# A recurrence woven into a layer stack: its input loads issued 16 steps earlier than before, the scaling of the inputs kept where it was

## The chip, the cores and the metric

The kernel runs on one core of a Trainium2 chip. A core has five engines that run at the same time, each taking its own instructions in order: TensorE (PE, with its weight loads shown as PEld), VectorE (DVE), ScalarE (ACT), GpSimd (POOL) and SyncE (SP). SP computes nothing here; it issues transfers between the chip's memory and the core's on-chip memory. An instruction that waits for another engine or for a transfer waits on a semaphore, and holds everything behind it on its own engine.

The metric is the device time in microseconds of one execution. Beside it there is one execution that was profiled, with its own time and the span from its first to its last instruction.

## The reference, cut to what matters

The model has two layers of the form "token mixer, then feed-forward part". What the change touches is the feed-forward part of layer 0, a recurrence over 4096 tokens for 4 batch entries and 128 channels:

```python
B, T, H = (x.shape[0], x.shape[1], W.shape[0])      # 4, 4096, 128
Wx = jnp.einsum('bti,hi->bth', x, W)
flat = Wx.reshape(B * T, H)
mean = jnp.mean(flat, axis=0)
var = jnp.var(flat, axis=0)
Wx = ((flat - mean) * jax.lax.rsqrt(var + BN_EPS) * gamma + beta).reshape(B, T, H)
def step(yt, wx_t):
    yt = jax.nn.sigmoid(wx_t + yt @ Vt)
    return (yt, yt)
_, ys = jax.lax.scan(step, y0, jnp.swapaxes(Wx, 0, 1))
```

Its result is added to the layer's input. The mixer of layer 1 takes the sum: eight layers of a selective state-space model (Mamba) over the same tokens, each with its own projections, a short convolution, a scan over the tokens for 256 channels and 16 states, and a gate:

```python
for l in range(DEPTH):                               # 8
    seq = _mamba_layer(seq, W_in[l], conv_w[l], ...)
    seq = _rmsnorm(seq, rms_w[l])
```

Before this stand the mixer of layer 0 (an attention over windows with sampled positions), and behind it the feed-forward part of layer 1 (a routed set of experts). Neither is touched.

## The kernel before, in words

The kernel keeps channels on the 128 partitions and tokens along the free dimension. Its order of work is written out by hand: each engine's instructions stand in the order in which the Python code issues them, and a framework adds the semaphore waits that the data need. Four parts follow each other: the attention mixer (`conv_layer`), the set-up and first steps of the recurrence, the eight Mamba layers with the rest of the recurrence woven in (`mamba`), and the experts.

**The recurrence** (class `Recurrence`, from L605). A group is 64 steps (`RT`). `load(n)` allocates two tiles of 128 x 4 x 64 numbers in fp32 from a pool of two buffers each, and issues two transfers on SP: `wx`, the projected inputs (L664), and `x1`, the layer's input that is added at the end (L666). Each reads 128 KB in runs of 256 bytes. At the end of `load` one ScalarE instruction (L667) scales and shifts `wx` by the batch statistics, in place. `step(t)` is a product of the state with the matrix V on TensorE (L683), into a PSUM tile that at the first step of a group was filled with the scaled inputs (L678). `tanh(t)` is a ScalarE instruction (L691) on 128 x 4 numbers that gives the next state. At the last step of a group POOL turns the states into outputs, writing them into the `wx` tile (L697), adds `x1` (L698), and SP stores the sum (L700).

**Where the loads stood.** `tanh(t)` called `load(n + 1)` at step 32 of group n, just after that step's tanh. So the two transfers and the scaling were issued together, and stood on SP and ScalarE at the place of step 32.

**The first 576 steps** (nine groups) run alone, each step waiting for the one before it. Small dummy products fill TensorE between them (L655).

**The eight layers.** The tokens are cut into eight chunks of 512. A *body* is one chunk, one layer and one batch entry: 8 x 8 x 4 = 256 bodies, batch entry innermost, so that body number modulo 4 is the batch entry b. A body has 16 slots, each with two scans on DVE (L1075) for one pair of states and one half of the channels. For these, ScalarE makes the decay factors `dA` (L1020), three slots ahead, and TensorE the inputs `dBx` (L1042), one slot ahead. POOL multiplies four states at a time by the C coefficients (L1100), and TensorE adds up the products (L1104). A table (`PLAN`) places the other pieces of the next body and the previous one: projections, convolution taps (L895, L898, L904), gates, norms (L838 to L841 for a chunk's first layer), stores and fetches.

Another table, `STEPS`, places 16 recurrence steps in each body, at most two in a slot. After the first 576 steps, 3520 remain, which takes 220 bodies. A group of 64 steps therefore spans exactly four bodies: step 0 falls on the first slot of a body with b=0, step 16 on that of b=1, step 32 on that of b=2.

**SP's queue in a body.** SP issues in this order: copies of the C coefficients, spread over all partitions, 1 MB each (`Cb`, L957, four for each body, of which the first two go out in the last slots of the body before it); the weights of the next layer at the start of bodies with b=1 (`given`, L828, 640 KB); and later in the body the small transfers that hold coefficients for the next body (L942, L1009), B (L950) and the spread diagonal (`diag`, L1014, 1.8 MB). In the last layer of a chunk there are also stores of the result (L1167), loads of the value it is added to (L1159), and the next chunk's inputs (L834).

Of the kernel before, what the change touches and what calls it, by code (L numbers as in the profile page):

```python
# [10 lines left out]
AF = mybir.ActivationFunctionType  # L11
# [12 lines left out]
L = H * W  # L24
# [30 lines left out]
RT = 64  # L55
# [6 lines left out]
class Ops:  # L62


    def __init__(self, nc, const):
        self.nc = nc
        self.ident = const.tile([P, P], F32, name="ident")
        make_identity(nc, self.ident)
        self.avg = const.tile([P, P], F32, name="avg")
        nc.vector.memset(self.avg, 1.0 / P)  # L70
        self.one = const.tile([P, 1], F32, name="one")
        nc.vector.memset(self.one, 1.0)
        self.eps5 = const.tile([P, 1], F32, name="eps5")
        nc.vector.memset(self.eps5, 1e-5)
        self.eps6 = const.tile([P, 1], F32, name="eps6")
        nc.vector.memset(self.eps6, 1e-6)
# [533 lines left out]
class Recurrence:  # L610
# [5 lines left out]
    def __init__(self, ctx, tc, ops, I, stats, wx_d, x1_d, x2_d):  # L616
        nc = self.nc = tc.nc
        self.ops, self.wx_d, self.x1_d, self.x2_d = ops, wx_d, x1_d, x2_d
        c = ctx.enter_context(tc.tile_pool(name="rc", bufs=1))
        self.w = ctx.enter_context(tc.tile_pool(name="rw", bufs=2))  # L620
        self.ps = ctx.enter_context(tc.tile_pool(name="rps", bufs=1, space=PSUM))
        vt = self.vt = c.tile([P, P], F32, name="vt")
        nc.sync.dma_start(out=vt, in_=I["V"])
        vec = c.tile([P, V_N], F32, name="vec")
        nc.sync.dma_start(out=vec, in_=I["vec"])
        nc.vector.tensor_scalar(vt, vt, 0.5, None, ALU.mult)
        mv = c.tile([P, 2], F32, name="mv")
        nc.vector.bn_aggr(mv, stats.rearrange("p n s -> p (n s)"))
        sc = self.sc = c.tile([P, 1], F32, name="sc")
        ops.rstd(sc, mv[:, 1:2], ops.eps5)  # L630
        nc.scalar.preload_act_table_set(EXP_TANH)
        nc.vector.tensor_tensor(sc, sc, vec[:, V_GAMMA : V_GAMMA + 1], ALU.mult)
        sh = self.sh = c.tile([P, 1], F32, name="sh")
        nc.vector.tensor_tensor(sh, mv[:, 0:1], sc, ALU.mult)
        nc.vector.tensor_tensor(sh, vec[:, V_BETA : V_BETA + 1], sh, ALU.subtract)
        self.still = c.tile([P, P], BF16, name="still")
        nc.gpsimd.memset(self.still, 0.0)
        idle = self.ps.tile([P, TL], F32, tag="p", name="idle")
        for _ in range(32):
            self.busy(idle, TL // P)  # L640
        half = self.ps.tile([P, RT, B], F32, tag="p", name="half")
        nc.tensor.matmul(half[:, 0, 0:1], vt, ops.one, start=True, stop=True)
        idle = self.ps.tile([P, TL], F32, tag="p", name="idle")
        for _ in range(6):
            self.busy(idle, TL // P)
        nc.vector.tensor_tensor(sh, sh, half[:, 0, 0:1], ALU.add)
        z0 = c.tile([P, B], F32, name="z0")
        nc.vector.memset(z0, -1.0)
        self.before = z0
        self.got = {}  # L650
        self.load(0)

    def busy(self, out, n):

        self.nc.tensor.matmul(  # L655
            out[:, : n * P].rearrange("p (n t) -> p n t", n=n), self.still,
            self.still.unsqueeze(1).to_broadcast([P, n, P]), start=True, stop=True,
        )

    def load(self, n):  # L660
        nc = self.nc
        here = (slice(None), slice(None), slice(n * RT, (n + 1) * RT))
        wx = self.w.tile([P, B, RT], F32, tag="wx", name="wx")
        nc.sync.dma_start(out=wx, in_=self.wx_d[here])  # L664
        x1 = self.w.tile([P, B, RT], F32, tag="x1", name="x1")
        nc.sync.dma_start(out=x1, in_=self.x1_d[here])  # L666
        nc.scalar.activation(wx, wx, AF.Identity, scale=self.sc, bias=self.sh)  # L667
        self.got[n] = wx, x1

    def step(self, t):  # L670

        nc = self.nc
        n, k = divmod(t, RT)
        if k == 0:

            self.wx, self.x1 = self.got.pop(n)
            self.p = self.ps.tile([P, RT, B], F32, tag="p", name="p")
            nc.tensor.matmul(  # L678
                self.p, self.ops.ident, self.wx.rearrange("p b t -> p t b"), start=True, stop=False,
                skip_group_check=True,  # L680
            )
            self.z = self.w.tile([P, RT, B], F32, tag="z", name="z")
        nc.tensor.matmul(  # L683
            self.p[:, k, :], self.vt, self.before, start=False, stop=True, skip_group_check=True
        )

    def tanh(self, t):

        nc = self.nc
        n, k = divmod(t, RT)  # L690
        nc.scalar.activation(self.z[:, k, :], self.p[:, k, :], AF.Tanh, scale=0.5)  # L691
        self.before = self.z[:, k, :]
        if k == RT // 2 and n + 1 < L // RT:
            self.load(n + 1)
        if k == RT - 1:
            y = self.wx
            nc.gpsimd.tensor_scalar(y, self.z.rearrange("p t b -> p b t"), 0.5, 0.5, ALU.mult, ALU.add)  # L697
            nc.gpsimd.tensor_tensor(self.x1, self.x1, y, ALU.add)  # L698
            here = (slice(None), slice(None), slice(n * RT, (n + 1) * RT))
            nc.sync.dma_start(out=self.x2_d[here], in_=self.x1)  # L700
# [46 lines left out]
def mamba(tc, ops, I, rec, x2_d, x3_d):  # L747
# [16 lines left out]
    with ExitStack() as ctx:  # L764
# [438 lines left out]
        def side(who, j, part):  # L1203

            for k, what in plan[j][part] if part < len(plan[j]) else ():
                if who.get(k):
                    pieces[what](who[k])

        load(0)
        idle = psf.tile([P, TL], F32, tag="f0", name="idle")  # L1210
        for t in range(PRE):
# [10 lines left out]
        for i in range(-2, len(bodies) + 1):  # L1222
# [7 lines left out]
            if o and o.b == 1 and i + 3 < len(bodies):  # L1230
                load(bodies[i + 3].l)
# [466 lines left out]
```

## Time and profile before

| What | Value |
|---|---|
| Time, median of 3 runs | 14895.22 us (14884.57 to 14900.8) |
| Profiled execution, its time | 14892.08 us |
| Profiled execution, span | 14890.3 us |
| Busy share of PE, DVE, ACT, POOL | 95%, 87%, 74%, 85% |
| Mean granted TensorE clock | 0.984 |
| First scan of the first body to last scan of the last | 1946 to 14607 us |
| L667, scaling | 64 executions, 0.60 us each |
| L664, load of wx: issue to landing, whole program | 2.5 / 7.4 / 13.5 us (min, median, max) |
| L666, load of x1: issue to landing, whole program | 2.4 / 7.2 / 12.7 us (min, median, max) |

The page gives busy time per engine, the span in 40 slices, the transfers, and the costliest groups of instructions. Views of the trace behind it give who waited for whom, the instructions in order of time, and busy times in chosen stretches. A busy share is an average over the stages. Idle time of an engine matters only where another engine, or the end, waits for it.

### The profile page before, as it was taken

Reading aid. Unit: us, or ns where it says so; the run is one execution under the profiler, and the core shown is the slowest. Engines: PE = TensorE matmul, PEld = TensorE weight load, DVE = VectorE, ACT = ScalarE, POOL = GpSimd, SP = SyncE. Lnnn points to the kernel's source line nnn. Section 1 sums busy time; section 2 is a strip of 40 time slices with the busy share of each in tenths; the row PEclk is TensorE's granted clock in tenths of the full one; section 3 lists DMA queues with packets and bytes.
Section 4 is the critical chain, followed back from the end, with each engine's and each line's share of the span. In section 5 each row is a group of like instructions: output and inputs, shape, how many; then the busy total and the mean of one; then the engine's idle time right before and its main releaser. Section 6 shows DMA issues by size and latency. Waiting matters only on the chain. (4 is left out here: it accounts for less than half of the span.)

```text
span 14890.3 us, 307789 instructions
## 1 busy us (share of the span) xinstructions
PE 14160.7 (95%) x124378; PEld 10821.2 (73%) x124378; DVE 12974.0 (87%) x16043; ACT 10980.2 (74%) x21400; POOL 12589.8 (85%) x5760
## 2 busy tenths in 40 slices
PE   7999989999999999999999999999999999999996
PEld 3444467777777777777777777777777777777775
DVE  8997079998999899999998999989999999989994
ACT  6887267777777777777777777777777777777773
POOL 5564079999999999999999999999999999999993
PEclk8999999999999999999999999999999999999998
DMA  0000034434443434343444344344434343434344
GB/s 23 26 26 23 29 122 144 144 136 148 142 147 135 152 137 150 132 151 138 149 142 144 137 149 142 138 145 145 146 136 151 138 149 133 154 131 145 133 146 184
DMA packets 600044, 1914.56 MB, mean 129 GB/s; under 512 B 347488, under 2 KB 347872, under 8 KB 434272
## 3 DMA queue, kind: packets, MB, share of 16 engines
q1 hardware_dynamic: 598480, 1894.60, 36.1%
q8 instruction: 984, 16.12, 0.4%
q14 instruction: 436, 3.57, 0.1%
q10 hardware_dynamic: 144, 0.26, 0.0%
HBM read 1823.10 MB, written 71.57 MB: 127 GB/s over the span
## 5 line engine op out<-in xcount | busy, mean ns | idle before, releaser
L1100 POOL TENSOR_TENSOR hs<-hs,Cb 128x2048 f32<-128x2048 f32 x2048 | 9300.9, 4543 | 749.0 <-DVE state L1092 562.3
L1075 DVE TENSOR_TENSOR_SCAN hs<-dA,state,dBx 128x512 f32<-128x512 f32 x7168 | 8808.2, 1267 | 700.2 <-PE dBx L1042 561.3
L1020 ACT ACTIVATE dA<-dt,A 128x512 f32<-128x512 f32 x7168 | 4730.4, 716 | 11.6 <-DVE hs L1075 5.5
L1104 PE MATMUL yT<-ident,hs 128*128 128x128 f32 x32768 | 4376.9, 277 | 30.4 <-POOL hs L1100 30.2
L1042 PE MATMUL dBx<-diag,dtxT 64*128 64x128 f32 x57344 | 4195.3, 283 | 27.1 <-DVE hs L1075 20.1
L1104 PEld LDWEIGHTS yT<-ident,hs 128*128 128x128 f32 x32768 | 3785.4, 147 | 433.6 <-issue 349.2
L1042 PEld LDWEIGHTS dBx<-diag,dtxT 64*128 64x128 f32 x57344 | 3509.4, 187 | 800.7 <-issue 741.3
L683 PEld LDWEIGHTS p<-z,vt 128*128 128x128 f32 x8192 | 1283.9, 189 | 881.8 <-ACT z L691 401.8
L691 ACT ACTIVATE z<-p 128x4 f32<-128x4 f32 x4096 | 702.3, 171 | 1396.6 <-PE p L683 1368.8
L683 PE MATMUL p<-z,vt 128*128 128x4 f32 x8192 | 1453.7, 248 | 107.1 <-ACT z L691 98.4
L1075 DVE TENSOR_TENSOR_SCAN hs<-dAp,state,hs 128x512 f32<-128x512 f32 x1024 | 1273.3, 1273 | 296.7 <-POOL hs L1063 296.7
L1063 POOL TENSOR_TENSOR hs<-Bb,dtx 128x512 f32<-128x512 f32 x1024 | 1284.9, 1280 | 0.0
L904 DVE SCALAR_TENSOR_TENSOR xc<-f,taps,xc 128x511 f32<-128x511 f32 (+2 forms) x1536 | 1115.8, 726 | 53.4 <-ACT z L691 49.3
L1020 ACT ACTIVATE dAp<-dt,A 128x512 f32<-128x512 f32 x1024 | 708.8, 692 | 491.6 <-DVE hs L1075 470.1
L279 DVE SCALAR_TENSOR_TENSOR acc<-qp,dww,acc 128x512 f32<-128x512 f32 x1184 | 892.4, 754 | 25.6
L979 POOL TENSOR_TENSOR dtx<-dt,xc 128x512 f32<-128x512 f32 x512 | 651.6, 1273 | 217.5 <-ACT dt L973 217.5
L293 POOL TENSOR_TENSOR off<-off,to 128x512 f32<-128x512 f32 x288 | 366.4, 1272 | 412.7 <-ACT to L291 400.0
L1020 ACT ACT_TABLE_LOAD x511 | 655.6, 1283 | 9.0
L898 ACT ACTIVATE xc<-f,taps 128x512 f32<-128x512 f32 x512 | 350.7, 685 | 414.7 <-PE f L895 281.1
L919 PE MATMUL f<-u,given 128*128 128x512 f32 x1024 | 600.6, 670 | 3.8 <-DVE xc L904 3.8
L847 PEld LDWEIGHTS f<-avg,sq 128*128 128x128 f32 x2048 | 257.0, 197 | 466.0 <-ACT sq L1148 466.0
L895 PE MATMUL f<-u,given 128*128 128x512 f32 x1024 | 567.0, 636 | 0.8 <-DVE u L868 0.8
(235 smaller groups left out, 15160.8 us busy)
## 6 DMA issues: line engine op xcount, KB each, us to landing
Cb<-c_d SPq DMA_DIRECT2D x1024, 1024.0 KB, 7.2
diag<-spare SPq DMA_DIRECT2D x256, 1792.0 KB, 8.8
Bb<-c_d SPq DMA_DIRECT2D x256, 512.0 KB, 4.8
given<-in_m_given_dram SPq DMA_DIRECT2D x64, 640.0 KB, 8.6
slab<-in_w_dram SPq DMA_DIRECT2D x60, 512.0 KB, 9.9
x<-x_d SPq DMA_DIRECT2D x96, 256.0 KB, 3.0
c_d<-dbl SPq DMA_DIRECT2D x512, 32.0 KB, 1.6
x_d<-x SPq DMA_DIRECT2D x63, 256.0 KB, 3.2
```

What stands on the lines that cost most here:

```text
L279: nc.vector.scalar_tensor_tensor(rows(to), x, dww[:, t : t + 1], rows(o.acc), ALU.mult, ALU.add)
L683: nc.tensor.matmul(self.p[:, k, :], self.vt, self.before, start=False, stop=True, skip_group_check=True)
L691: nc.scalar.activation(self.z[:, k, :], self.p[:, k, :], AF.Tanh, scale=0.5)
L904: nc.vector.scalar_tensor_tensor(x, o.v[h][:, : TL - k], taps[:, o.l, h, DC - 1 - k : DC - k], x, ALU.mult, ALU.add)
L919: nc.tensor.matmul(o.pz[h], o.given[:, at : at + P], o.u, start=True, stop=True)
L979: nc.gpsimd.tensor_tensor(to, blocks(o.dt[h]), blocks(o.xc[:, h, :]), ALU.mult)
L1020: nc.scalar.activation(o.dA[j][:, k, :], o.dt[h], AF.Exp, scale=A[:, o.l, h, n : n + 1])
L1042: nc.tensor.matmul(o.dBx[j][:, at : at + 64, :], o.dtxT[h][row, n, :], o.diag[row, n, :, 2 * sp : 2 * sp + 2], start=True, stop=True,)
L1063: nc.gpsimd.tensor_tensor(hs[:, k, :].rearrange("p (q n t) -> p q n t", n=NB, q=2), o.Bb[:, k, :].rearrange("p (q n t) -> p q n t", n=NB, ...
L1075: nc.vector.tensor_tensor_scan(hs[:, k, :], o.dA[j][:, k, :], hs[:, k, :] if sp == SP_B else o.dBx[j][:, :, k], state[:, o.l, o.b, h, s : ...
L1100: nc.gpsimd.tensor_tensor(hs, hs, o.Cb[f], ALU.mult)
L1104: nc.tensor.matmul(o.yT[:, n, :], x[:, n * P : (n + 1) * P], ops.ident, start=start and n == 0, stop=True, is_transpose=True, skip_group_c ...
```

## The change

`load` no longer ends with the scaling. The scaling is a function of its own, `scale(n)`. The constructor calls both, one after the other, for group 0. In the steps, `load(n + 1)` is called at step 16 of a group and `scale(n + 1)` at step 32.

```diff
         self.load(0)
+        self.scale(0)
...
         x1 = self.w.tile([P, B, RT], F32, tag="x1", name="x1")
         nc.sync.dma_start(out=x1, in_=self.x1_d[here])
-        nc.scalar.activation(wx, wx, AF.Identity, scale=self.sc, bias=self.sh)
         self.got[n] = wx, x1
+
+    def scale(self, n):
+        wx = self.got[n][0]
+        self.nc.scalar.activation(wx, wx, AF.Identity, scale=self.sc, bias=self.sh)
...
         self.before = self.z[:, k, :]
-        if k == RT // 2 and n + 1 < L // RT:
-            self.load(n + 1)
+        if n + 1 < L // RT:
+            if k == RT // 4:
+                self.load(n + 1)
+            if k == RT // 2:
+                self.scale(n + 1)
```

## The prediction

> **What bounds the kernel now.** I read the page first: its rows of engines and slices show a kernel that is nearly full from 1946 us on, so only time that stops several engines at once can be won. Then I read the waits of ScalarE (ACT), because the change touches what ACT waits for. Columns: engine and tile, "<-" what it waited for, total us, times, longest us. Over the eight-layer stage (window 1900 to 12900 us, the whole part in which recurrence steps are woven into the layers):
>
> ```profile
> ACT z L691 <- PE p L683: 1090.6, 1532, 6.6
> ACT dAp L1020 <- DVE hs L1075: 304.3, 405, 3.2
> ...
> ACT wx L667 <- DMA wx<-wx_d: 88.3, 45, 7.5
> ```
>
> The third line is the scaling at step 32: 45 of its 54 executions here wait for the load issued just ahead of them, 88.3 us in all. Over the window before (1490 to 1900 us, the steps alone) the only wait of L667 is the set-up's:
>
> ```profile
> ACT wx L667 <- DVE z L648: 2.3, 1, 2.3
> ```
>
> There SP has nothing else to do and has issued each load as soon as its buffer was free, long before ACT comes to it. So those nine loads can give nothing.
>
> An ACT wait is not yet lost time. I therefore cut the stage into bodies, from one body's first scan (L1075) to the next one's. A body holds 16 steps, so the load at step 32 always falls on the third body of a layer (b=2), and step 16 on the second (b=1). Lengths from the trace: b=1 and b=3 take 48.57 us in layers 0 to 6 and 50.70 us in layer 7 (which also prepares the next chunk), nearly without exception. Bodies b=2 do not. Five stretches (length, busy time per engine with counts, granted clock of PE, DMA share, GB/s):
>
> ```profile
> 3418.18:3477.28 59.10, 52.50 (x460) 42.58 (x459) 46.57 (x55) 38.67 (x75) 47.30 (x21) 0.94 0.39 136
> 3477.28:3527.98 50.70, 49.71 (x460) 40.04 (x459) 46.55 (x55) 38.29 (x74) 47.25 (x21) 1.00 0.43 150
> 5553.03:5601.63 48.60, 47.58 (x446) 38.35 (x445) 45.14 (x52) 37.78 (x73) 45.15 (x19) 1.00 0.42 156
> 5601.63:5650.20 48.57, 47.55 (x446) 38.34 (x445) 45.12 (x52) 38.26 (x74) 45.11 (x19) 1.00 0.41 140
> 2631.68:2682.93 51.25, 49.19 (x446) 39.20 (x445) 45.33 (x52) 38.06 (x74) 45.09 (x19) 0.97 0.38 134
> ```
>
> Rows 1 and 2 are b=2 and b=3 of one layer 7: same work, 8.40 us apart. Row 4 is a b=2 whose load was in time (wait 0), as long as row 3, its neighbour without a load; the 0.60 us of the scaling itself is hidden, ACT being busy 38 of 48.6 us. Row 5 is a b=2 with a wait of 2.07 us. In the long ones PE's clock was granted at 0.94 and 0.97 in place of 1.00, so the idle stretch also slows PE afterwards. This is why a body can lose more than ACT waited.
>
> Why the load is late stands in the order of time of the b=2 of row 1 (SP's issues, then ACT's work; start, length, instruction):
>
> ```profile
> 3415.74 0.32 SPq L1159 DMA_DIRECT2D x<-x_d  x1
> 3416.11 0.43 SPq L834 DMA_DIRECT2D x<-x_d  x1
> 3416.59 0.90 SPq L957 DMA_DIRECT2D Cb<-c_d  x2
> 3417.53 0.57 SPq L664 DMA_DIRECT2D wx<-wx_d  x1
> ...
> 3428.13 0.60 ACT L667 ACTIVATE wx<-wx,sh,sc 128x256 f32<-128x256 f32 x1 [7.50 <-DMA wx<-wx_d]
> ...
> 3429.98 0.75 DVE L904 SCALAR_TENSOR_TENSOR xc<-f,taps,xc 128x511 f32<-128x511 f32 x1 [5.50 <-ACT z L691]
> ```
>
> The load goes out behind two 1 MB copies of C (L957) and lands 0.5 us after the second of them, 10.6 us after its issue. ACT stands at L667 and holds the activations behind it: L841, L898, the next tanh and the dA exponentials. DVE then idles 5.50 us for the L898 result. In layers 0 to 6 the load is issued 3.9 us before the body, its C copies in front of it, and lands at +1.5 to +4.5 us; ACT reaches L667 at +2.35.
>
> **The change, part by part.**
> *Removed: the wait of L667.* The instruction keeps its place on ACT at step 32. Its load will have gone out at about -3.5 us of b=1, and ACT reaches L667 at +2.35 of b=2: 54 us later (48.6 + 5.9). The slowest landing of L664 in this stage, 11.3 us from issue, leaves 43 us of that.
> What that is worth, body by body (length of each loaded b=2 less its floor):
> - Layers 0 to 6, 48 bodies, floor 48.57. In the 23 with a wait under 1 us the mean excess is 0.00: the queue of prepared exponentials absorbs it. In the 11 with 1 to 1.5 us it is 0.87 us, in the 14 with more, 1.35 us: 11 x 0.87 + 14 x 1.35 = 28.5.
> - Layer 7, 6 bodies, floor 50.70 (their b=1 and b=3): 59.10 + 59.72 + 57.66 + 61.22 + 60.42 + 57.52 - 6 x 50.70 = 51.4. Waits there: 5.9 to 7.5 us.
> - Together 79.9 us. That it comes near the 88.3 of the wait row is chance: short waits cost nothing, long ones more than their length.
>
> *Added: one method call; no instruction.* In program order both kernels have the same instructions at the same places on PE, ACT, DVE and POOL; on SP 54 pairs of L664 and L666 stand one body earlier, behind the weight load `given` (L828), ahead of the third C copy. The round of eight DMA semaphores shifts, so that some instructions name another predecessor; each named one was issued eight transfers earlier and has landed.
>
> *Moved: two issues on SP.* They take SP 1.2 us in b=1 as a rule (0.57 and 0.63), 2.9 at worst (1.25 and 1.64), from 3.5 us before the body. SP's next is the C copy at +0.7 us, which waits for POOL anyway, so nothing behind them is late. Neither waits at its new place: the buffers come free with POOL's L698 and the store L700, which is landed by +7.5 us of body b=0 at the latest, over 40 us ahead. No POOL queue is passed.
>
> *Moved: 256 KB of transfers.* In b=1 they stand behind `given` and ahead of C copy 3. I bound what they push back: from nothing (C copy 3 lands at +6.7 us behind them in b=2, at +7.0 without them in b=3) to 1 us (x1 lands 0.46 us behind wx, so twice that). C copy 3 in b=1 lands at +8.0 and is used by POOL at +19.9, with at least 10.3 us of room; copy 4 at least 13.7. I take nothing. In b=2 the C copies lose this traffic, which matters to nobody.
>
> **A rule against the rows.** The Trainium skill, "DMA: Bandwidth & Descriptors", section "Anatomy of one DMA — SWDGE (gpsimd) path", fits a transfer as 2.0 us plus bytes over 436 GB/s (for that path; this is SP's). For 131072 bytes I estimate 2.3 us. Issued 3.9 us before the body, wx would land at -1.6 and nobody would wait: by the rule the change is worth almost nothing outside layer 7, and there (issue at -0.65, landing at +1.7, ACT at +2.45) nothing either, so 14895. With an empty queue the trace agrees (2.5 us at best), but in this stage the row says 5.4/7.5/11.3 us (min, median, max). The same page's "Queues, rings and completion order" says why: each DMA engine takes its descriptors in ring order, and here 2 MB of C stand ahead. The row decides.
>
> **Sum.** Profiled execution: span 14890.3, time 14892.1. Less 79.9: span 14810.4, time 14812.2. The median of the runs is 3.1 above the profiled time: 14895.2 - 79.9 = 14815.3.
>
> **Rivals.**
> 1. *Part of the layer-7 gain stays away* (14840 to 14866). There the C copies 1 and 2 themselves are late in b=2, since L1159 has to wait for a store to land (issue at -2.4, landing of copy 1 up to +6.6 us). With ACT freed POOL wants copy 1 at +8.4, so the room shrinks to 1.8 us. If another wait took that place, up to 51.4 would remain lost: 14866. Against it: b=3 of layer 7 has the same late copies (up to +6.3) and takes 50.70.
> 2. *No change* (within 30 us, about 14890): the time is lost elsewhere and the wait only displays it. Against: excess is zero in every body with no wait or a short one.
> 3. *Slower, crowding in b=1.* The moved loads use 256-byte runs; the same page ("Specifications") sets 512 bytes as the least for full rate. If they held up C copy 3 by more than its 10.3 us of room, POOL would stall in each of 54 bodies. Two us past that point is 108 us, a net 28 slower (14923); the break-even is 11.8 us of delay. The 0.46 us between wx and x1 speaks against it, but the mix with `given` is untried.
> 4. *More gain* (14790 to 14805): the 36 bodies after the last step run in an irregular pattern (48.3 to 51.4 us) that a different entry could shift by some 10 to 20 us, either way.
>
> **How the numbers follow.** Likeliest case 0.79, with its own range 14805 to 14830; rival 1 0.09, rival 2 0.04, rival 3 0.04, rival 4 0.04. A change of 0.2% (30 us) is about what can be told from no change. The low end takes in part of rival 4 and the high end most of rival 1: 14800 to 14845. Faster (likeliest, rival 4, most of rival 1) 0.91; within 0.2% 0.05; slower 0.04.
>
> **What would show it.** L667's wait for the DMA gone; b=2 at 48.57 and 50.70 us with PE's clock at 1.00; b=1 unchanged; wx landing at about +6 us of b=1. The forecast is wrong if b=1 grows, if a wait on POOL's C copies appears, or if layer-7 b=2 bodies stay above 51 us.

## The result

The changed kernel takes 14814.31 us (median of 4 runs, 14813.63 to 14817.47); the kernel before takes 14893.86 us (median of 4, one run more than above). The ratio is 0.9948, with a 95% interval of 0.9932 to 0.9964: faster by 79.6 us, about half a per cent. The forecast was 14815.3.

In lines of `kernel.py` the change moves what stands behind it: the scaling L667 is now L672, the loads L664 and L666 are L665 and L667, the tanh L691 is L695, the C copies L957 are L964. (The class of the recurrence begins at L610; the description above gives L605.)

ScalarE's waits in the changed kernel over the layers (window 1900 to 12900 us; columns: what waited, for what, total us, times, longest us):

```profile
ACT z L695 <- PE p L687: 1096.3, 1563, 6.9
ACT dAp L1027 <- DVE hs L1082: 294.9, 403, 3.2
ACT dbl L946 <- PE f L940: 251.9, 224, 2.4
```

The first two stand where they stood (1090.6 and 304.3 us). The 88.3 us of the scaling are gone; it has no row any more. What stood behind it shows on DVE. In the same window, the waits of the convolution's taps for ScalarE's result, before:

```profile
DVE xc L904 <- ACT z L691: 49.3, 73, 5.5
```

and after:

```profile
DVE xc L911 <- ACT z L695: 9.5, 48, 0.5
```

Next come four bodies of the changed kernel that answer to those shown of the one before (length, busy time per engine, granted clock, DMA share, GB/s). The first two are b=2 and b=3 of the first layer 7, the last two b=1 and b=2 of a middle layer:

```profile
3415.94:3466.67 50.73, 49.74 (x460) 40.05 (x459) 46.57 (x55) 38.78 (x75) 47.29 (x21) 1.00 0.44 149
3466.67:3517.37 50.70, 49.72 (x460) 40.07 (x459) 46.55 (x56) 38.32 (x74) 47.24 (x21) 1.00 0.43 150
5531.11:5579.70 48.59, 47.57 (x446) 38.35 (x445) 45.13 (x52) 37.78 (x73) 45.14 (x19) 1.00 0.43 155
5579.70:5628.26 48.56, 47.54 (x446) 38.34 (x445) 45.10 (x52) 38.26 (x74) 45.11 (x19) 1.00 0.39 140
```

The body of 59.10 us is now one of 50.73, with PE's clock at 1.00 throughout. ScalarE's work in it is the same: 38.78 us of activity, against 38.67.

In order of time the same stretch reads as follows (SP's issues at the start of b=1 and of b=2, then ScalarE's):

```profile
3361.36 0.43 SPq L835 DMA_DIRECT2D given<-in_m_given_dram  x1
3361.84 0.56 SPq L665 DMA_DIRECT2D wx<-wx_d  x1
3362.44 0.63 SPq L667 DMA_DIRECT2D x<-x_d  x1
...
3413.66 3.29 SPq L964 DMA_DIRECT2D Cb<-c_d  x3
...
3418.23 0.17 ACT L695 ACTIVATE z<-p 128x4 f32<-128x4 f32 x1 [0.89 <-PE p L687]
3418.30 0.59 ACT L672 ACTIVATE wx<-wx,sh,sc 128x256 f32<-128x256 f32 x1
```

The loads go out right behind the weights, 56 us ahead of the scaling. The C copies of b=2 still come late, but the scaling follows its tanh without a gap.

Over all 54 loaded groups, bodies b=2 now take 48.57 us in layers 0 to 6 (48.55 to 48.59) and 50.81 in layer 7 (50.70 to 51.23). Cut the spans at the first scan and at the body after the last step: of the difference of 74.6 us between the two profiled spans (14890.3 and 14815.7), b=2 gave 79.2, the other bodies of this stretch took back 2.5, the part ahead of the first body took 2.9 more, and the remaining 36 bodies and the experts gave 0.8. So the bodies b=2 account for the whole gain.

### The profile page after: what moved, and what is told of

Read it like the earlier page. It is cut to its first block, busy times and chain, and to the rows that moved or that the text cites. A ratio compares the mean times of both kernels' runs of the same rounds, so it can differ in the third digit from the quotient of the medians.

```text
span 14815.7 us, 307842 instructions
## 1 busy us (share of the span) xinstructions
PE 14124.4 (95%) x124378; PEld 10790.5 (73%) x124378; DVE 12971.0 (88%) x16043; ACT 10985.9 (74%) x21400; POOL 12590.3 (85%) x5760
## 5 line engine op out<-in xcount | busy, mean ns | idle before, releaser
L695 ACT ACTIVATE z<-p 128x4 f32<-128x4 f32 x4096 | 703.1, 172 | 1403.9 <-PE p L687 1374.6
```

## The experiments

Times are medians; the kernel before took 14891 to 14899 us beside them. Where a body's excess is named, it is its length less 48.57 us, or less 50.70 us in layer 7. The diffs are against the changed kernel, except the seventh, which is against the kernel before; they show the lines that matter, with constants written as numbers.

**1. The loads stay, the scaling moves.** This parts the wait from the traffic.

```diff
-            if k == RT // 4:
+            if k == RT // 2:
                 self.load(n + 1)
-            if k == RT // 2:
+            if k == 3 * RT // 4:
                 self.scale(n + 1)
```

> Both loads stay at step 32, as in the kernel before; only the scaling moves, to step 48. Theory (time is lost where ScalarE stands at the scaling until wx has landed, and nowhere else): the wait is gone, bodies b=2 take 48.57 us in layers 0 to 6 and 50.7 in layer 7, b=3 the same; 14815 us, give or take 10. Rival A (the gain comes from moving 256 KB of transfers out of b=2): the traffic stays, so about 14890. Rival B (the C copies in layer 7 hold b=2 up by themselves): b=2 of layer 7 stays above 55 us, some 14865.

Measured: 14811.25 us (ratio 0.9944, 0.9927 to 0.9960). All b=2 bodies are at their floors (48.58 and 50.72 on average), and b=3, where the scaling now stands, too. The transfers are where they always were, so it was not their traffic (rival A) and not the late C copies of layer 7 (rival B).

**2. Only the awaited load moves.** The load of x1 is split from `load` into a function of its own, called at step 32:

```diff
             if k == RT // 2:
+                self.load_x1(n + 1)
                 self.scale(n + 1)
```

> As after the change, but x1, which nobody waits for before the end of its group, is loaded at step 32 again; wx alone at step 16. Theory: 14815 us, no wait of the scaling. Rival A (moved traffic): half of it is back in b=2, so half of the gain is lost, about 14855.

Measured (one run): 14812.82 us, b=2 at 48.61 and 50.71. That x1 moves along does nothing, for good or ill.

**3. Load and scaling both at step 16.**

```diff
-            if k == RT // 2:
+            if k == RT // 4:
                 self.scale(n + 1)
```

> Load and scaling both at step 16: the change without its second half. Theory: wx lands at about +5.2 us of b=1, behind the second C copy and the weights, ScalarE comes to it at +2.35, so it waits some 2.9 us in each of 54 bodies. From the waits above 1.5 us in the kernel before, such a wait costs 1.4 to 2.9 us: 75 to 155 us on top of 14815, likeliest 14930; layer 7 costs no more than other layers, since its queue is not late in b=1. Rival A (moved traffic): 14815.

Measured: 15044.85 us (ratio 1.0099, 1.0084 to 1.0114), slower than the kernel before. The mechanism is as expected in the layers: wx lands at +5.3 us, ScalarE waits 2.78 us on average, and 54 bodies b=1 lose 134 us in all. One of them, of layer 7 (floor 50.7 us), with a wait of 2.82 us:

```profile
3470.84:3525.56 54.72, 52.80 (x460) 42.72 (x459) 46.58 (x55) 38.67 (x75) 47.26 (x21) 0.94 0.37 128
```

But 96 us more are lost ahead of the first body (it begins at 2042.1 us, in the kernel before at 1945.6), which was not expected. Experiments 9 and 10 take these up.

**4. One step earlier: 31.**

```diff
-            if k == RT // 4:
+            if k == RT // 2 - 1:
                 self.load(n + 1)
```

> Loads one step earlier than in the kernel before (31), scaling at 32. On SP they now stand ahead of the second C copy and behind the first. Theory (ring order): in layers 0 to 6 wx lands at about -1 us of b=2, no wait. In layer 7 SP comes late to both, wx lands behind the first C copy at about +6, ScalarE waits some 4 us, 4 to 6 us lost in each of 6 bodies: 14815 plus 24 to 36, about 14845. Rival C (one step is too little, the load needs its 7.5 us and more from any place): 14880 or more.

Measured: 14842.27 us (0.9964, 0.9951 to 0.9977). In layers 0 to 6 wx lands at -0.5 us, no body b=2 waits, and they are all at 48.58. In layer 7 it lands at +6.3. ScalarE's row for it, over the layers:

```profile
ACT wx L672 <- DMA wx<-wx_d: 22.4, 6, 4.3
```

Six waits of 3.73 us on average cost 5.2 us each, 31 in all. SP's issues and ScalarE's scaling in the first of these bodies:

```profile
3411.71 0.42 SPq L964 DMA_DIRECT2D Cb<-c_d  x1
3412.18 0.57 SPq L665 DMA_DIRECT2D wx<-wx_d  x1
...
3420.12 0.60 ACT L672 ACTIVATE wx<-wx,sh,sc 128x256 f32<-128x256 f32 x1 [3.73 <-DMA wx<-wx_d]
```

One C copy stands ahead of the load instead of two, and the wait is 3.7 in place of 7.5 us. Over the six bodies the mean time from issue to landing falls from 10.4 to 8.0 us. In layers 0 to 6 it grows instead, from 7.4 to 10.1 us (medians), because at the earlier place the spread diagonal and B are still under way in front of it. There the load is in time only because it goes out 6.7 us earlier. Here and in the kernel before it lands about 0.5 us (median) behind the C copy issued just before it, and in the changed kernel 0.5 us behind the weights. What decides is how much lies in front of the load at the time of its issue, and when that is.

**5. A busy ScalarE in place of a waiting one.**

```diff
                 self.scale(n + 1)
+                for _ in range(4 if t >= PRE else 0):
+                    nc.scalar.activation(
+                        self.dummy, self.got[n + 1][0].rearrange("p b t -> p (b t)"), AF.Copy, scale=0.5
+                    )
```

> As after the change, with four more ScalarE instructions of 128x256 (0.4 to 0.6 us each, some 2 us in all; their result is not used) behind the scaling at step 32 in the layers. The cost of a busy ScalarE at this place by itself, with no wait for a transfer. Theory: as a wait of 2 us cost in the kernel before, about 1.35 us in each of 54 bodies, 14888 us (14870 to 14910). Rival A (ScalarE has 10 us to spare in a body and it was the traffic): 14815.

Measured: 14869.77 us (0.9981, 0.9971 to 0.9990 against the kernel before), so 55 us over the changed kernel. The time lies just below the range expected: the four instructions took 0.418 us each, 1.67 in all, less than assumed, and layer 7 lost nothing (50.72). In layers 0 to 6 the b=2 bodies lose 1.08 us on average. They fall into two groups: 37 lose 0.73 us with PE's clock at 1.00, and 11 lose 2.2 to 2.3 with the clock at 0.97. One of each:

```profile
3022.11:3071.41 49.30, 47.62 (x446) 38.36 (x445) 45.24 (x52) 39.63 (x78) 45.10 (x19) 1.00 0.39 135
2824.71:2875.51 50.80, 49.12 (x446) 39.21 (x445) 45.34 (x52) 39.63 (x78) 45.09 (x19) 0.97 0.36 134
```

So ScalarE's time at this place costs by itself, with no transfer behind it and some 10 us of idle ScalarE time in the body, and the lower clock costs 1.5 us on top where it falls. But 1.67 us of work in layer 7 is wholly absorbed, so the point below which nothing is lost is not the same in all layers.

**6. More of the moved traffic.**

```diff
         self.got[n] = wx, x1
+        for i in range(8 if n * RT > PRE else 0):
+            nc.sync.dma_start(out=self.more[i], in_=(self.wx_d, self.x1_d)[i % 2][here])
```

> As after the change, with eight more copies of 128 KB in 256-byte runs behind each pair of loads at step 16 (to scratch in the chip's memory, unused): 1.25 MB in 256-byte runs where the change has 0.25. Theory: SP issues the third C copy of b=1 at about +3 in place of +0.7, and it lands at +12 to +15; it is used at +19.9, so 14815 again. Rival D (crowding in b=1): some us lost in 54 bodies, over 14850.

Measured: 14816.04 us (0.9946, 0.9929 to 0.9963): no loss. SP needed longer for the issues than thought, so the third C copy of b=1 went out at +8.0 us, not +3, and landed at +14.3. POOL wanted it at +19.9, with at least 3.4 us left.

**7. TensorE kept at work during the long waits.** Against the kernel before:

```diff
+        if k == RT // 2 + 1 and t >= PRE and (t - PRE) // 64 % 8 == 7:
+            for _ in range(80):
+                nc.tensor.matmul(
+                    self.p[:, k + 1 :, :].rearrange("p t b -> p (t b)"), self.still,
+                    self.still[:, 0 : (RT - k - 1) * B], start=False, stop=True, skip_group_check=True,
+                )
```

> The kernel before, with 80 small products of zeros (128x120, added to the accumulators) on TensorE behind step 33 in the six b=2 bodies of layer 7 that carry a load, where TensorE stands idle for 5.6 us. Theory (a long wait costs more than its length because TensorE's clock is halved after the idle stretch): these bodies fall from 59.3 to about 56.5 us, the granted clock in them from 0.94 to 1.00, 14878 us in all. Rival E (clock is a symptom): they stay at 59 us or grow.

Measured (one run): 14880.16 us. The six bodies take 55.72 us on average, against 59.27; their waits were 6.23 us, against 6.56. Four of them:

```profile
3423.29:3478.86 55.57, 53.91 (x540) 44.23 (x539) 46.60 (x55) 38.66 (x75) 47.25 (x21) 1.00 0.44 145
4999.68:5054.45 54.77, 53.79 (x540) 44.21 (x539) 46.65 (x55) 38.67 (x75) 47.28 (x21) 1.00 0.41 142
6577.40:6632.23 54.83, 53.85 (x540) 44.24 (x539) 46.59 (x55) 38.66 (x75) 47.23 (x21) 1.00 0.41 135
8156.67:8213.88 57.21, 55.43 (x540) 45.51 (x539) 46.60 (x55) 38.68 (x75) 47.33 (x21) 0.97 0.41 138
```

There are 80 matmuls more, and the bodies are shorter. In four of the six the clock stayed at 1.00: they lose 4.3 us for a mean wait of 5.9. In the other two, with the longest waits (6.9 us), it still fell, to 0.97, and they lose 6.5. In the kernel before, the stretch behind such a wait looked thus (idle, then the work after it):

```profile
3424.00:3430.00 6.00, 0.39 (x8) 0.19 (x4) 0.50 (x2) 1.87 (x6) 0.55 (x1) 0.93 1.06 391
3430.00:3434.00 4.00, 4.00 (x18) 3.70 (x18) 3.86 (x6) 2.45 (x5) 1.80 (x1) 0.50 0.33 135
3434.00:3438.00 4.00, 4.00 (x35) 3.57 (x34) 1.83 (x2) 1.21 (x4) 3.92 (x4) 0.75 0.00 0
```

After 5.6 us without work TensorE ran at a granted 0.50. With the products between, an excess of 8.57 us for a wait of 6.56 becomes, on average over all six, one of 5.02 for 6.23. So the clock accounts for some 3 us of each of these bodies.

**8. The break-even of crowding.** As 6, with 24 copies.

> As the run with eight more copies, with 24. Theory: SP needs some 14 us more for them, so the third C copy of b=1 is issued at +12 and lands at +18 to +24, around the time at which POOL wants it (+19.9): 0 to 4 us lost in each of some 53 bodies, 14815 to 15030, likeliest 14900, and a wait of POOL on a C copy shows. If nothing is lost here either, the room in b=1 is larger than read from the trace.

Measured (one run): 15138.49 us, beyond the range expected. POOL's row over the layers:

```profile
POOL hs L1112 <- DMA Cb<-c_d: 296.5, 52, 8.3
```

SP spent 21 us on the issues, not 14; the third C copy of b=1 went out at +19.3 and landed at +25.7, 5.8 us after POOL would have taken it. The bodies b=1 lose about that: 6.0 us on average in layers 0 to 6, 5.5 in layer 7, 320 in all. The mechanism of the slower rival exists. The change stays far from it.

**9 and 10. What one short wait did before the layers.** Number 9 is number 3 with the scaling of the first 576 steps left at step 32; number 10 is the changed kernel with one scaling moved, that for the second group:

```diff
-            if k == RT // 2:
+            if k == (RT // 4 if n == 0 else RT // 2):
                 self.scale(n + 1)
```

> As the run with load and scaling both at step 16, but in the first 576 steps the scaling stays at step 32. That run lost 96 us in the first 576 steps, where TensorE's clock stood at half from 1518 to about 1885 us. Theory: with the scaling at 32 there this loss is gone, and the one in the layers (waits of 2.8 us, 2.5 us lost in each of 54 bodies) stays: about 14950 us. Rival F (the 96 us come with step 16 itself or with chance): 15045.

> As after the change, but the scaling for the second group alone is done at step 16 of the first; all other scalings at step 32. One ScalarE instruction moved by 16 steps. Theory: its load lands only at 1518 us, behind the set-up's transfers, ScalarE waits about 1.9 us, TensorE stands idle for that time, its clock falls to half and stays there for the rest of the lone steps: 14814 plus about 96, 14910 us. Rival F: 14816, a wait of 2 us costs 2 us.

Number 9 (one run): 14929.23 us; the first body begins at 1945.9 us again, so the 96 us are gone, and the b=1 bodies lose 118. Number 10: 14940.14 us, the median of ten runs. That is 126 us more than the changed kernel, from one ScalarE instruction placed 16 steps earlier. It is more than the 96 expected. Seven of the runs lie at 14938 to 14942, three at 14837, 14868 and 14874. In the profiled one, the wait:

```profile
1519.32 0.60 ACT L672 ACTIVATE wx<-wx,sh,sc 128x256 f32<-128x256 f32 x1 [1.37 <-DMA wx<-wx_d]
```

and TensorE from there on (columns as for the bodies):

```profile
1516.00:1521.00 5.00, 3.62 (x22) 1.96 (x21) 0.00 (x0) 1.37 (x7) 0.00 (x0) 1.00 0.44 133
1530.00:1700.00 170.00, 170.00 (x683) 109.40 (x684) 0.00 (x0) 34.50 (x195) 4.13 (x6) 0.50 0.03 8
1700.00:1990.00 290.00, 290.00 (x1164) 186.42 (x1163) 0.00 (x0) 60.26 (x336) 6.87 (x10) 0.50 0.03 7
```

The changed kernel in the second of these stretches:

```profile
1530.00:1700.00 170.00, 166.21 (x909) 86.39 (x907) 0.00 (x0) 46.28 (x261) 5.49 (x8) 1.00 0.04 10
```

A wait of 1.4 us left TensorE idle for 1.3, and its clock fell to half at 1522.4 us. It stayed there for 522 us; in the 460 us shown of these TensorE is recorded as busy all the time. What were 261 ScalarE instructions in 170 us, nearly all of them tanh, are now 195. Rival F (a wait of 2 us costs 2 us) is out. The three faster runs fit: their mean granted clock is 0.979 to 0.984, that of the seven others 0.969 or 0.970, that of the changed kernel 0.986 or 0.987. In number 3 the clock fell at 1520.5 us, after 1.8 us of idleness, and came back at 1899.4; here it stayed low to the end of the lone steps.

## Why the prediction was right

**The wait (removed).** Right, as shown by experiment 1: only the distance between load and scaling counts. Two ways of making it long, by an earlier load or a later scaling, give the same time within the runs.

**Its worth, body by body.** Forecast 79.9 us, found 79.2 in the b=2 bodies. That the medians meet the forecast to 1 us is luck: in the profiled runs whose lone steps ran at full clock, the part ahead of the first body alone takes anything from 1942.6 to 1951.3 us. The floors were read right: the neighbours' lengths and the 23 bodies with short waits told what a b=2 takes. That the total comes near the 88.3 us of the row is chance, as the prediction said: experiment 3 loses 134 us for 150 us of waits and experiment 4 loses 31 for 22.

**Why long waits cost more than their length.** The prediction put it down to TensorE's clock from two rows. Experiment 7 shows it: keep TensorE's clock up, and the bodies lose less than the wait instead of more. The Trainium skill has the rule ("TensorE: Matmul & The Clock Gate", Part 1): the clock falls to half after an idle window of about 3.4 us. Here 5.6 us of idleness did it, in agreement. But the same trace shows the clock fall after far less, and the prediction lumped this into its averages for layers 0 to 6. In the kernel before, 8 of these 48 bodies have a clock of 0.97. Two bodies with nearly the same wait (2.10 and 2.07 us; the second is row 5 of the prediction):

```profile
7377.66:7427.39 49.73, 47.64 (x446) 38.36 (x445) 45.24 (x53) 38.09 (x74) 45.10 (x19) 1.00 0.40 139
2631.68:2682.93 51.25, 49.19 (x446) 39.20 (x445) 45.33 (x52) 38.06 (x74) 45.09 (x19) 0.97 0.38 134
```

In the second one, the stretch before the clock fell and the one after:

```profile
2654.33:2657.75 3.42, 2.53 (x18) 2.05 (x18) 2.99 (x4) 3.40 (x7) 3.42 (x2) 1.00 0.02 5
2657.75:2661.16 3.41, 3.41 (x19) 1.90 (x17) 2.52 (x3) 2.63 (x4) 3.41 (x4) 0.50 0.00 0
```

TensorE had been idle for 0.89 of 3.42 us. Such a fall adds about 1.5 us, so that some 12 of the 28.5 us of layers 0 to 6 are the clock's. Other bodies with the same pause kept their clock; what decides between them stays open.

**Why short waits cost nothing.** The prediction named the prepared exponentials. Experiment 5 confirms that there is such a cushion on ScalarE's time, and that its depth differs: all of 1.67 us in layer 7, 0.94 of it in the bodies of the other layers that kept their clock. The kernel before has the same depth in layers 0 to 6. There, with the clock at 1.00, a body loses its wait less about 0.95 us: nothing up to 0.97 us, 0.14 for 1.09, 1.15 for 2.10. That it consists of the exponentials made ahead was argued, not shown.

**The ring order against the fixed price.** Right. The fit of 2.3 us would have given no gain. Experiment 4 settles it: the same load, with the same bytes, waits about half as long in layer 7 with one C copy ahead of it instead of two (3.7 us on average, against 6.6). That it waits not at all in the other layers is due to its earlier issue alone, since it takes longer to land there.

**The two issues and the 256 KB moved.** Taken as nothing; found nothing: b=1 is 48.65 us in layers 0 to 6 (48.61 before), and the third C copy lands at +8.3, where +8.0 to +9.0 was allowed, with the same 10.3 us of room at the least. One body b=1 (3568.8 to 3619.3 us) is 1.9 us longer than in the kernel before. Its granted clock is 0.97: it stood at 0.50 for 3.4 us, as in the cases above; why it fell in this body stays open. wx lands at +5.2 us of b=1 (forecast about +6).

**The rivals.** The first, part of the layer-7 gain lost to late C copies, did not come. One layer-7 body is 0.5 us over its floor (51.23 us, above the 51 that the prediction had named as a sign of being wrong), but in it TensorE waited for the next chunk's input:

```profile
4990.06 1.10 PE L845 MATMUL f<-x,avg 128*128 128x512 f32 x2 [0.37 <-DMA x<-x_d]
```

A row of POOL waiting for C copies appears too, with 2.1 us in three waits of 0.69, and such a wait was another such sign. But it is no wait for C: the copy used there had landed 9 us earlier, and POOL pauses for 0.69 us at the same place in nearly every body b=1 of both kernels. The slower rival needed 11.8 us of delay to the C copy; experiment 6 delays it by 6.0 without loss, experiment 8 by 17.4 with some 6 us lost per body. The irregular 36 bodies at the end took 1792.4 us, against 1793.5.

## What to carry to other kernels

An in-order engine that waits for a load pays at the place of the wait, not at the load: look for the instruction that first reads it, and put distance between the two, by moving either. How early is early enough is read from what lies ahead on the transfer queue (here up to 2 MB), not from the load's own size. And price a stall by the bodies around it rather than by the length of the wait: in layers 0 to 6 here the first microsecond was free, while a wait of little more could also cost TensorE's clock, 1.5 us for a short fall and some 3 after the long waits. Look at the granted clock of each body before laying its excess to the wait.

## What was not expected of the hardware

A single idle stretch of 1.3 us on TensorE, in a phase of short dependent steps with filler products between them, was followed by a granted clock of one half for 522 us, while for at least 460 of them the records show TensorE busy without a gap. The rule of the page named above has the clock return after one busy window of about 3.4 us, and fall after an idle one. By it I would estimate a loss of a few microseconds, if the clock fell at all; the runs lost about 126 us in seven of ten. In the layers the clock did return after one to four such steps of 3.41 us, much as the page has it, but it fell there after 0.89 us of idleness in 3.42. The measurement decides here. What brought the clock back in experiment 3, and what kept the loss of the other three runs at 23 to 59 us, stays open. The changed kernel escapes it because in these steps its scaling still stands at step 32, when the load has long landed: moving the scaling along with the load, the simpler edit, would have made the kernel 1% slower than it was.
